# Neighbour sums from PSUM on VectorE, and copies that GpSimd may take

## The chip, the cores and the metric

The kernel runs on one core of a Trainium2 chip. A core has five engines that run side by side and meet at semaphores: TensorE (PE in the profile; PEld is its weight load), VectorE (DVE), ScalarE (ACT), GpSimd (POOL) and SyncE (SP), which here issues the transfers. TensorE writes its results to PSUM, where this kernel has eight tiles of 128 x 512 float32; VectorE and ScalarE read PSUM and the on-chip memory SBUF. The metric is device time in microseconds of one execution; lower is better.

## What is computed

The input is `x` (128 graphs x 128 nodes x 256 features, float32) and `adj` (128 x 128 x 128 integers). Four layers follow one another, each of the form `x = layernorm(x + layer(x, adj))`.

Layer 0 is a gated graph network with three steps:

```
A = (adj != 0)
h = x
for i in range(3):
    m = einsum('bnd,de->bne', h, weight[i])
    aggr = einsum('bst,bsd->btd', A, m)        # neighbour sum
    h = gru_cell(aggr, h, w_ih, w_hh, b_ih, b_hh)
```

The cell forms `gi = aggr @ w_ih.T + b_ih` and `gh = h @ w_hh.T + b_hh`, each three times 256 wide, then `r = sigmoid(i_r + h_r)`, `z = sigmoid(i_z + h_z)`, `n = tanh(i_n + r * h_n)` and `h = (1 - z) * n + z * h`.

Layers 1 to 3 are attention layers: `Wh = x @ W.T`, a score for each pair of nodes from two vectors, leaky ReLU, a mask by `adj`, softmax over the neighbours, and the weighted sum of `Wh`.

## The kernel before

**Tiling.** Four graphs make a group (`G = 4`), so there are 32 groups. Nodes, or features in two halves of 128 (`KC = 2`), lie on the 128 partitions, and a tile's row is usually `GN = 512` float32: four graphs x 128. For each group `gru` does layer 0 and `gat` layers 1 to 3. The product of the adjacency with `h` is formed first (the neighbour sum, L702 in bfloat16 parts or L705 in float32), and the two weight matrices `weight[i]` and `w_ih` are multiplied with each other once near the start (L459), so that a step has two products: hidden state with `whs`, neighbour sum with `wcs[i]`.

**The gates.** These products (`strassen`, matmuls on L639) use Strassen's scheme on 2 x 2 blocks: seven block products instead of eight, whose operands are the blocks themselves or sums of blocks. On the weights' side the sums are made once. On the data's side `sums` makes four tiles of 128 x 256 for the hidden state and four for the neighbour sum, in every step of every group (L608): `second - first`, then `fourth - part(0)`, `fourth - second`, and `part(1) - third`. The second block product of a set waits for all four. The accumulators (`gate`, five PSUM banks) are emptied on the way by `whole` (L716) and `halves` (L720, L723) on ScalarE and by `add` (L644) on VectorE. Then come the nonlinear functions on ScalarE (L734, L747, L763) and the elementwise chain on VectorE and partly GpSimd (L750 to L773).

**The neighbour sum.** Each half is multiplied into one of the three PSUM banks for everything else (`bank`) and copied to SBUF by ScalarE or VectorE (`EVICT`; these instructions carry the lines L404 and L406 of the helper `copy`). `sums` reads these copies.

**Transposes.** Where a tile is turned through the transfer engines' crossbar (`turned`, a DMA transpose of 16-bit elements), float32 words have to be split into 16-bit halves before (`APART`, L404 and L406) and put together after (`TOGETHER`, L503 on ScalarE, L406 on VectorE): 396 such copies of 128 x 1024 in a run. `thirds` splits the hidden state into three bfloat16 parts for the next neighbour sum: roundings (`ROUND`, `copy`) and rests (L528), then crossbar transposes. The last four groups (`LAST = 4`) do without the crossbar and use TensorE's transposes (L803, L860, L907); their stages run side by side at the end of the program.

**Attention.** Scores come from L831 on VectorE, a transpose (L843), a broadcast on GpSimd (L850), a sum with the mask and a maximum (L866), ScalarE's L870 and L887, a transpose of the weights and their scaling (L897, L899), then two products (L937, L948), whose result L954 adds to the layer's input. L555 is a power on GpSimd for the norms, and L582 sums squares.

**Order.** `Plan` is a list scheduler that runs while the program is built. Every operation has the engines that may do it, with a price in ns for each, a priority from its group and stage (`stage`, `LATER`) and buffers from pools with a fixed number of slots. `Plan.order` simulates the engines several times, the later times with due times from the time before, and keeps the shortest plan; the engines' instructions are then issued in that order. Constants in it are `RUSH` (priority of operations that read PSUM), `RATHER` (when GpSimd leaves work to VectorE), `MARGIN` (how long TensorE's operations are kept back after their operands are due from another engine) and `own` (slots that a group's half keeps for itself). Operations with `port=BOTH` are kept apart from each other on VectorE and GpSimd.

Of the kernel before, what the change touches and what calls it, by code (L numbers as in the profile page):

```python
# [20 lines left out]
GN = G * P  # L21
H = GN // 2
# [28 lines left out]
class Plan:  # L51
# [8 lines left out]
             ("ACT", "POOL"): 190, ("ACT", "ACT"): 145, ("DVE", "PE"): 140, ("DVE", "ACT"): 120, ("DVE", "POOL"): 165,  # L60
             ("DVE", "DVE"): 120, ("POOL", "POOL"): 115, ("POOL", "ACT"): 95, ("POOL", "DVE"): 95}

    RUSH = 0.25
    RATHER = 600
    MARGIN = 300

    def __init__(self, slots, own):
        self.free = {t: list(range(n)) for t, n in slots.items()}
# [240 lines left out]
def adj_resnorm_kernel(  # L309
# [14 lines left out]
    nc = tc.nc  # L324
# [9 lines left out]

    pools = {"gru": 4, "xs": 2, "am": 5, "k2": 27, "k4": 18, "f": 3, "mv": 4, "st": 6, "v": 36,
             "mb": 4, "gate": 5, "bank": 3}
    own = ({"k2": 7, "k4": 10, "gate": 0, "bank": 0, "v": 5, "st": 0}, {"k2": 3, "k4": 2, "bank": 0, "v": 4, "st": 0})
    floats = {"gru": 0, "k4": 1024, "xs": 1024, "f": 128, "mv": 8, "st": 6, "v": 4, "mb": GN // 2}
    tags = {t: (n, floats.get(t, 512)) for t, n in pools.items()}
    U16, BF16 = mybir.dt.uint16, mybir.dt.bfloat16  # L340
    BOTH = ("DVE", "POOL")
    LATER = (0.25, 1.75, -1.0, 0.25, 0, -0.5)
    plan = Plan({t: n for t, (n, _) in tags.items()}, own)
    slots = {t: [(psum if t in ("gate", "bank") else work).tile([P, w], F32, name=f"{t}{i}")
                 for i in range(n)] for t, (n, w) in tags.items() if w}
# [1 line left out]
    def T(b):  # L347
        if b.at is None:
            width = 1
            for s in b.shape:  # L350
                width *= s
            at = slots[b.tag][b.slot][:, 0:width]
            if len(b.shape) == 2:
                at = at.rearrange("p (a b) -> p a b", b=b.shape[-1])
            elif len(b.shape) == 3:
                at = at.rearrange("p (a b c) -> p a b c", b=b.shape[-2], c=b.shape[-1])
            b.at = at
        return b.at

    def bank():  # L360
        return Buf("bank", GN)
# [17 lines left out]
    whs = here(consts.tile([P, 7, 3, P], F32, name="whs"))  # L379

    wcs = [here(consts.tile([P, 7, 3, P], F32, name=f"wcs{i}")) for i in range(STEPS)]
# [20 lines left out]
    def copy(e, dst, src):  # L402
        if e == "ACT":
            nc.scalar.copy(dst, src)  # L404
        else:
            nc.vector.tensor_copy(dst, src)  # L406

    LAND = 1500
    EVICT = {"ACT": 475, "DVE": 602}
    APART = {"ACT": 938, "DVE": 602}  # L410
    TOGETHER = {"ACT": 1058, "DVE": 602}
    TURN = -1800
    EVICT2 = {"ACT": 370, "DVE": 350}
    ROUND = {"ACT": 475, "DVE": 335}

    def load(dst, src, prio, start=0):

# [177 lines left out]
                reads=[(ss, b) for b in range(G)] + [eps], writes=[ve], prio=prio, port=BOTH)  # L595
        return ve

    def sums(ms, prio):

        t = Buf("k4", 4, H)  # L600
        first, second = (lambda: T(ms[0])[:, 0:H]), (lambda: T(ms[0])[:, H:GN])
        third, fourth = (lambda: T(ms[1])[:, 0:H]), (lambda: T(ms[1])[:, H:GN])
        part = lambda j: lambda: T(t)[:, j, :]
        for j, (a, b, reads) in enumerate((
                (second, first, [ms[0]]), (fourth, part(0), [ms[1], (t, 0)]), (fourth, second, ms),
                (part(1), third, [ms[1], (t, 1)]))):
            plan.op({"POOL": 690, "DVE": 335}, lambda e, j=j, a=a, b=b: (
                nc.vector if e == "DVE" else nc.gpsimd).tensor_tensor(T(t)[:, j, :], a(), b(), ALU.subtract),  # L608
                reads=reads, writes=[(t, j)], prio=prio, port=BOTH)
        return t  # L610

    def moving(m, ms):
# [52 lines left out]
    def gru(g, stage):  # L665

        xs, am = Buf("xs", G, D), Buf("am", G, P)
        prio = stage(g, 0)
# [4 lines left out]
                writes=[am], prio=prio)  # L673
        if g == 0:
# [3 lines left out]
                reads=[am], writes=[am, turn], prio=prio, port=BOTH)  # L678
        by_thirds = g < NG - LAST
        if by_thirds:  # L680
            low = Buf("mb", GN // 2)
            narrow = lambda b: T(low).bitcast(BF16)[:, b * P:(b + 1) * P]
        if g < 2:
            hT = transposed(xs, lambda b, c: T(xs)[:, b, c * P:(c + 1) * P], prio)
        else:
            hT = [Buf("k2", GN) for c in range(KC)]
            for c in range(KC):
                turned(lambda c=c: T(xs)[:, :, c * P:(c + 1) * P], [xs], hT[c], prio)
        h = None
        for i in range(STEPS):  # L690
            prio = stage(g, i)
            if g == 0 and i > 0:
                input_weights(i, (prio[0], -2))
            agg = []
            for c in range(KC):
                b_, a_ = bank(), Buf("k2", GN)

                def fn(e, b_=b_, c=c, h=h):
                    for b in range(G):
                        if by_thirds and h is not None:  # L700
                            for j in (2, 1, 0):
                                nc.tensor.matmul(T(b_)[:, b * P:(b + 1) * P], h[1](c, b, j), narrow(b), start=j == 2, stop=j == 0)  # L702
                            continue
                        src = T(xs)[:, b, c * P:(c + 1) * P] if h is None else T(h[c])[:, b, :]
                        nc.tensor.matmul(T(b_)[:, b * P:(b + 1) * P], src, T(am)[:, b, :], start=True, stop=True)  # L705
                if by_thirds and h is not None:
                    plan.op({"PE": 12 * 55.6}, fn, reads=[low, h[0][c], h[0][2]], writes=[b_], prio=prio, room=[a_])
                else:
                    plan.op({"PE": 4 * 222.7}, fn, reads=[am, xs if h is None else h[c]], writes=[b_], prio=prio, room=[a_])
                plan.op(EVICT, lambda e, b_=b_, a_=a_: copy(e, T(a_), T(b_)), reads=[b_], writes=[a_], prio=prio)  # L710
                agg.append(a_)
            last = i == STEPS - 1
            h_in, a_in = (whs, (hT, sums(hT, prio))), (wcs[i], (agg, sums(agg, prio)))

            def whole(dst, src, c):
                plan.op({"ACT": 475}, lambda e: nc.scalar.copy(T(dst), T(src)),  # L716
# [12 lines left out]
            for c in range(KC):  # L729

                o, v, d = rz[c], nn[c], Buf("k2", GN)
# [57 lines left out]
            for c in range(KC):  # L789
# [9 lines left out]
                b_ = bank()  # L799
# [223 lines left out]
```

## Time and profile before

| what | before |
|---|---|
| time, median of 3 runs | 2498.13 us (2497.54 to 2498.33) |
| the profiled execution's own time | 2499.11 us |
| its span, first to last instruction | 2497.3 us |
| TensorE busy | 2466.9 us (99%) |
| VectorE busy | 2200.0 us (88%) |
| ScalarE busy | 1896.6 us (76%) |
| GpSimd busy | 1099.4 us (44%) |
| DMA | 161.39 MB, of it 366 crossbar transposes |

The profile shows one execution. A row of its groups has the source line, the engine, the operation, output and inputs by tile name (`k` stands for all work tiles of the pools `k2` and `k4`), shapes and count, then the busy time in us, the mean of one in ns, and the engine's idle time ahead of these instructions with what ended most of it. A line can be that of a helper: all of `copy` is L404 (ScalarE) or L406 (VectorE). A float32 matmul shows as two records.

### The profile page before, as it was taken

The page shows a single profiled execution, that of the slowest core. Times are in us where ns is not written, and L with a number is a line of the kernel's source. Part 1 is how long each engine was busy: PE and PEld are TensorE (multiplying, and loading weights), DVE is VectorE, ACT ScalarE, POOL GpSimd, SP SyncE. Part 2 cuts the span into 40 slices and gives each one's busy share as a digit, 9 for nine tenths or more (in the row PEclk, how much of TensorE's full clock was granted, in tenths as well). Part 3 has the DMA queues.
Part 4 walks back from the last instruction along what each step waited for, and adds up shares of the span by engine and source line. Part 5 has one row for each costly group of instructions (what it writes and reads, how often), then busy time and mean ns, then how long its engine had stood idle before and what let it go on. Part 6 is the DMA issues. An engine that isn't in the chain of part 4 may idle for free. (4 is left out here: it accounts for less than half of the span.)

```text
span 2497.3 us, 42426 instructions
## 1 busy us (share of the span) xinstructions
PE 2466.9 (99%) x13492; PEld 2182.1 (87%) x13492; DVE 2200.0 (88%) x6167; ACT 1896.6 (76%) x4798; POOL 1099.4 (44%) x1312
## 2 busy tenths in 40 slices
PE   9999999999999999999999999999999999999998
PEld 7888888888888888888888888888888888888877
DVE  6888888989989999989988989999999998887887
ACT  5667777878888777777787877777777777776578
POOL 3434445555354543445545445444345543333211
PEclk9999999999999999999999999999999999999999
DMA  5222332333233332433333333232323332210101
GB/s 148 53 54 58 74 75 53 73 72 73 64 85 69 70 74 48 89 76 60 77 68 56 86 66 70 65 84 60 77 60 72 77 72 52 56 26 18 39 1 35
DMA packets 456610, 161.39 MB, mean 65 GB/s; under 512 B 389184, under 2 KB 454720, under 8 KB 456384
## 3 DMA queue, kind: packets, MB, share of 16 engines
q1 hardware_dynamic: 455952, 158.65, 29.6%
q8 instruction: 106, 1.74, 0.3%
q14 instruction: 120, 0.98, 0.1%
q10 hardware_dynamic: 432, 0.01, 0.0%
HBM read 45.89 MB, written 16.78 MB: 25 GB/s over the span
## 5 line engine op out<-in xcount | busy, mean ns | idle before, releaser
L639 PE MATMUL gate<-k,whs 128*128 128x256 f32 x4032 | 1206.5, 381 | 6.0 <-DVE k L644 2.6
L639 PE MATMUL gate<-k,wcs 128*128 128x256 f32 x4032 | 1199.3, 379 | 0.6 <-ACT wcs L404 0.6
L639 PEld LDWEIGHTS gate<-k,wcs 128*128 128x128 f32 x4032 | 766.0, 190 | 105.1 <-ACT wcs L404 1.0
L639 PEld LDWEIGHTS gate<-k,whs 128*128 128x128 f32 x4032 | 740.9, 190 | 111.9 <-DVE k L644 6.9
L644 DVE TENSOR_TENSOR k<-gate,k 128x512 f32<-128x512 f32 x576 | 391.9, 684 | 112.4 <-PE gate L639 85.1
L608 POOL TENSOR_TENSOR k<-k,k 128x256 f32<-128x256 f32 x474 | 399.2, 857 | 174.8 <-ACT k L404 55.9
L555 POOL TENSOR_TENSOR v<-v,neghalf 128x4 f32<-128x4 f32 x128 | 148.8, 1163 | 476.8 <-DVE v L593 232.4
L948 PE MATMUL bank<-gwT,k 128*128 128x256 f32 x1536 | 350.4, 381 | 0.8 <-DVE k L406 0.4
L831 DVE SCALAR_TENSOR_TENSOR nobody<-k,wa 128x256 bf16<-128x256 f32 x768 | 336.9, 471 | 2.7 <-ACT k L574 2.3
L948 PEld LDWEIGHTS bank<-gwT,k 128*128 128x128 f32 x1536 | 289.8, 190 | 41.8 <-DVE k L406 1.7
L608 POOL TENSOR_TENSOR k<-k 128x256 f32<-128x256 f32 x164 | 146.2, 893 | 372.1 <-DVE k L773 107.7
L734 ACT ACTIVATE k<-k,brz 128x512 f32<-128x512 f32 (+1 forms) x384 | 226.3, 623 | 73.9 <-DVE k L644 73.5
L716 ACT COPY k<-gate 128x512 f32<-128x512 f32 x288 | 167.4, 582 | 116.9 <-PE gate L639 113.7
L404 ACT COPY k<-bank 128x512 f32<-128x512 f32 (+1 forms) x283 | 151.0, 536 | 89.6 <-PE bank L843 30.3
L582 ACT ACTIVATE nobody<-k 128x256 bf16<-128x256 f32 x384 | 156.3, 410 | 70.5 <-DVE k L954 69.7
L850 POOL PARTITION_BROADCAST k<-k x336 | 154.1, 558 | 124.4 <-ACT k L404 66.0
L503 ACT COPY k<-k 128x1024 uint16<-128x1024 uint16 x153 | 177.4, 1162 | 33.9 <-DMA k<-k 33.5
L768 POOL TENSOR_TENSOR k<-k,k 128x512 f32<-128x512 f32 x89 | 119.7, 1347 | 188.0 <-ACT k L763 172.7
L954 DVE SCALAR_TENSOR_TENSOR k<-bank,v,k 128x256 f32<-128x256 f32 x384 | 167.4, 476 | 36.1 <-PE bank L948 34.3
L937 PEld LDWEIGHTS bank<-k,k 128*128 128x128 f32 x1536 | 187.8, 193 | 8.6 <-ACT k L503 1.7
L937 PE MATMUL bank<-k,k 128*128 128x128 f32 x1536 | 190.3, 277 | 2.6 <-ACT k L404 1.2
L763 ACT ACTIVATE k<-k,bi 128x512 f32<-128x512 f32 x192 | 137.1, 721 | 39.4 <-DVE k L760 20.2
(109 smaller groups left out, 3472.4 us busy)
## 6 DMA issues: line engine op xcount, KB each, us to landing
xs<-in_x_dram SPq DMA_DIRECT2D x32, 512.0 KB, 4.1
k<-in_x_dram SPq DMA_DIRECT2D x32, 512.0 KB, 4.2
out_dram<-k SPq DMA_DIRECT2D x32, 512.0 KB, 3.0
am<-in_adj_dram SPq DMA_DIRECT2D x32, 256.0 KB, 2.9
k<-k SPq DMA_TRANSPOSE x366, 3.1
k<-in_gnn_wT_dram SPq DMA_DIRECT2D x3, 256.0 KB, 4.9
k<-in_w_ihT_dram SPq DMA_DIRECT2D x2, 384.0 KB, 5.6
k<-in_w_hhT_dram SPq DMA_DIRECT2D x2, 384.0 KB, 6.4
```

Of the source, the lines that this page charges most:

```text
L503: nc.scalar.copy(flat().bitcast(U16).rearrange("p (q h) -> p q h", h=2), T(rows).bitcast(U16).rearrange("p (h q) -> p q h", h=2))
L582: plan.op({"ACT": 400}, lambda e, b=b: nc.scalar.activation(next(nobody[0]), T(y)[:, b, :], AF.Square, accum_out=T(ss)[:, b:b + 1]), reads ...
L608: nc.vector if e == "DVE" else nc.gpsimd).tensor_tensor(T(t)[:, j, :], a(), b(), ALU.subtract),
L639: nc.tensor.matmul(T(dst)[:, j * H:(j + 1) * H], T(w)[:, m, gt, :], moving(m, ms)[1](), start=first and n == 0, stop=n == len(todo) - 1, s ...
L644: plan.op({"DVE": 602}, lambda e: nc.vector.tensor_add(T(o)[:, :, j * H:(j + 1) * H], T(b_).rearrange("p (g n) -> p g n", g=2), T(part).re ...
L716: plan.op({"ACT": 475}, lambda e: nc.scalar.copy(T(dst), T(src)), reads=[src], writes=[(dst, 0), (dst, 1)], prio=prio)
L734: nc.scalar.activation(T(o)[:, gt, n0:n1], src(), AF.Tanh, bias=brz[:, gt * KC + c:gt * KC + c + 1], scale=0.5)
L831: plan.op({"DVE": 345}, lambda e, b=b, h=h, l=l, side=side, xc=xc: nc.vector.scalar_tensor_tensor(next(nobody[1]), T(xc)[:, b, :], 1.0, T( ...
L850: plan.op({"POOL": 292}, lambda e, row=row, b=b, e_=e_: nc.gpsimd.partition_broadcast(T(e_)[:, b, :], T(row)[b * P // G:b * P // G + 1, 0: ...
L937: nc.tensor.matmul(T(b_)[:, b * P:(b + 1) * P], T(xc)[:, b, c * P:(c + 1) * P], T(pT)[:, b, :], start=True, stop=True)
L948: nc.tensor.matmul(T(b_)[:, (b - b0) * D:(b - b0 + 1) * D], T(aT[k])[:, b * P:(b + 1) * P], T(gwT)[:, l, k, :], start=(k == 0), stop=(k == ...
L954: nc.vector.scalar_tensor_tensor(T(y)[:, b, :], T(b_)[:, (b - b0) * D:(b - b0 + 1) * D], T(rden)[:, b:b + 1], T(xc)[:, b, :], op0=ALU.mult ...
```

## The change

`sums` for the neighbour sum now takes its operands from the PSUM banks, apart from the two halves of the first bank where they are subtracted from another operand in PSUM: those come from the copy in SBUF. Only VectorE may do it, without `port=BOTH`, and the tile of sums is allocated together with the matmul. The sums of the hidden state are as before. `copy` gets a GpSimd branch, and the planner may give GpSimd the copies around the crossbar (price 1250) and the roundings to bfloat16 (price 700). Four planner constants differ: `RUSH`, `MARGIN`, one entry of `LATER`, and the `k4` slots of the second half in `own`. Since the planner orders the whole program, the order of instructions differs on every engine. Line numbers after the change are higher: by 2 from `copy` to `sums`, by 3 or 4 from there to the neighbour sum's matmuls, by 5 below.

```diff
--- before.py
+++ after.py
@@ -60,9 +60,9 @@
              ("ACT", "POOL"): 190, ("ACT", "ACT"): 145, ("DVE", "PE"): 140, ("DVE", "ACT"): 120, ("DVE", "POOL"): 165,
              ("DVE", "DVE"): 120, ("POOL", "POOL"): 115, ("POOL", "ACT"): 95, ("POOL", "DVE"): 95}
 
-    RUSH = 0.25
+    RUSH = 1.0
     RATHER = 600
-    MARGIN = 300
+    MARGIN = 200
 
     def __init__(self, slots, own):
         self.free = {t: list(range(n)) for t, n in slots.items()}
@@ -334,12 +334,12 @@
 
     pools = {"gru": 4, "xs": 2, "am": 5, "k2": 27, "k4": 18, "f": 3, "mv": 4, "st": 6, "v": 36,
              "mb": 4, "gate": 5, "bank": 3}
-    own = ({"k2": 7, "k4": 10, "gate": 0, "bank": 0, "v": 5, "st": 0}, {"k2": 3, "k4": 2, "bank": 0, "v": 4, "st": 0})
+    own = ({"k2": 7, "k4": 10, "gate": 0, "bank": 0, "v": 5, "st": 0}, {"k2": 3, "k4": 1, "bank": 0, "v": 4, "st": 0})
     floats = {"gru": 0, "k4": 1024, "xs": 1024, "f": 128, "mv": 8, "st": 6, "v": 4, "mb": GN // 2}
     tags = {t: (n, floats.get(t, 512)) for t, n in pools.items()}
     U16, BF16 = mybir.dt.uint16, mybir.dt.bfloat16
     BOTH = ("DVE", "POOL")
-    LATER = (0.25, 1.75, -1.0, 0.25, 0, -0.5)
+    LATER = (0.25, 1.75, -1.0, 0.25, -0.5, -0.5)
     plan = Plan({t: n for t, (n, _) in tags.items()}, own)
     slots = {t: [(psum if t in ("gate", "bank") else work).tile([P, w], F32, name=f"{t}{i}")
                  for i in range(n)] for t, (n, w) in tags.items() if w}
@@ -402,16 +402,18 @@
     def copy(e, dst, src):
         if e == "ACT":
             nc.scalar.copy(dst, src)
+        elif e == "POOL":
+            nc.gpsimd.tensor_copy(dst, src)
         else:
             nc.vector.tensor_copy(dst, src)
 
     LAND = 1500
     EVICT = {"ACT": 475, "DVE": 602}
-    APART = {"ACT": 938, "DVE": 602}
-    TOGETHER = {"ACT": 1058, "DVE": 602}
+    APART = {"ACT": 938, "DVE": 602, "POOL": 1250}
+    TOGETHER = {"ACT": 1058, "DVE": 602, "POOL": 1250}
     TURN = -1800
     EVICT2 = {"ACT": 370, "DVE": 350}
-    ROUND = {"ACT": 475, "DVE": 335}
+    ROUND = {"ACT": 475, "DVE": 335, "POOL": 700}
 
     def load(dst, src, prio, start=0):
 
@@ -595,18 +597,20 @@
                 reads=[(ss, b) for b in range(G)] + [eps], writes=[ve], prio=prio, port=BOTH)
         return ve
 
-    def sums(ms, prio):
-
-        t = Buf("k4", 4, H)
-        first, second = (lambda: T(ms[0])[:, 0:H]), (lambda: T(ms[0])[:, H:GN])
-        third, fourth = (lambda: T(ms[1])[:, 0:H]), (lambda: T(ms[1])[:, H:GN])
+    def sums(ms, prio, banks=None, t=None):
+
+        t = t or Buf("k4", 4, H)
+        at = banks or ms
+        first, second = (lambda: T(ms[0])[:, 0:H]), (lambda: T(at[0])[:, H:GN])
+        third, fourth = (lambda: T(at[1])[:, 0:H]), (lambda: T(at[1])[:, H:GN])
+        kept = lambda: T(ms[0])[:, H:GN]
         part = lambda j: lambda: T(t)[:, j, :]
         for j, (a, b, reads) in enumerate((
-                (second, first, [ms[0]]), (fourth, part(0), [ms[1], (t, 0)]), (fourth, second, ms),
-                (part(1), third, [ms[1], (t, 1)]))):
-            plan.op({"POOL": 690, "DVE": 335}, lambda e, j=j, a=a, b=b: (
+                (second, first, [at[0], ms[0]]), (fourth, part(0), [at[1], (t, 0)]), (fourth, kept, [ms[0], at[1]]),
+                (part(1), third, [at[1], (t, 1)]))):
+            plan.op({"DVE": 335} if banks else {"POOL": 690, "DVE": 335}, lambda e, j=j, a=a, b=b: (
                 nc.vector if e == "DVE" else nc.gpsimd).tensor_tensor(T(t)[:, j, :], a(), b(), ALU.subtract),
-                reads=reads, writes=[(t, j)], prio=prio, port=BOTH)
+                reads=reads, writes=[(t, j)], prio=prio, port=() if banks else BOTH)
         return t
 
     def moving(m, ms):
@@ -691,9 +695,10 @@
             prio = stage(g, i)
             if g == 0 and i > 0:
                 input_weights(i, (prio[0], -2))
-            agg = []
+            agg, banks, t = [], [], Buf("k4", 4, H)
             for c in range(KC):
                 b_, a_ = bank(), Buf("k2", GN)
+                banks.append(b_)
 
                 def fn(e, b_=b_, c=c, h=h):
                     for b in range(G):
@@ -704,13 +709,13 @@
                         src = T(xs)[:, b, c * P:(c + 1) * P] if h is None else T(h[c])[:, b, :]
                         nc.tensor.matmul(T(b_)[:, b * P:(b + 1) * P], src, T(am)[:, b, :], start=True, stop=True)
                 if by_thirds and h is not None:
-                    plan.op({"PE": 12 * 55.6}, fn, reads=[low, h[0][c], h[0][2]], writes=[b_], prio=prio, room=[a_])
+                    plan.op({"PE": 12 * 55.6}, fn, reads=[low, h[0][c], h[0][2]], writes=[b_], prio=prio, room=[a_, t])
                 else:
-                    plan.op({"PE": 4 * 222.7}, fn, reads=[am, xs if h is None else h[c]], writes=[b_], prio=prio, room=[a_])
+                    plan.op({"PE": 4 * 222.7}, fn, reads=[am, xs if h is None else h[c]], writes=[b_], prio=prio, room=[a_, t])
                 plan.op(EVICT, lambda e, b_=b_, a_=a_: copy(e, T(a_), T(b_)), reads=[b_], writes=[a_], prio=prio)
                 agg.append(a_)
             last = i == STEPS - 1
-            h_in, a_in = (whs, (hT, sums(hT, prio))), (wcs[i], (agg, sums(agg, prio)))
+            h_in, a_in = (whs, (hT, sums(hT, prio))), (wcs[i], (agg, sums(agg, prio, banks, t)))
 
             def whole(dst, src, c):
                 plan.op({"ACT": 475}, lambda e: nc.scalar.copy(T(dst), T(src)),
```

## The prediction

> **What bounds the kernel now.** I read the page's busy shares first, then the lengths of pieces in the chain that ended last, then TensorE's waits in the steady middle, then who waits for the instructions that move. The busy shares and two of the groups:
>
> ```profile
> PE 2466.9 (99%) x13492; PEld 2182.1 (87%) x13492; DVE 2200.0 (88%) x6167; ACT 1896.6 (76%) x4798; POOL 1099.4 (44%) x1312
> ...
> L608 POOL TENSOR_TENSOR k<-k,k 128x256 f32<-128x256 f32 x474 | 399.2, 857 | 174.8 <-ACT k L404 55.9 <-DVE k L773 48.3 <-DVE k L406 18.3
> ...
> L608 POOL TENSOR_TENSOR k<-k 128x256 f32<-128x256 f32 x164 | 146.2, 893 | 372.1 <-DVE k L773 107.7 <-ACT k L404 79.7 <-DVE k L406 73.7
> ```
>
> TensorE is the bound, but its 99% is not its floor, because matmul records overlap. The chain shows long unbroken pieces, which give the pace:
>
> ```profile
> 1839.66 15.54 PE gate L639 x72
> 1855.20 1.78 PE bank L937 x16
> 1856.99 1.73 PE gate L639 x8
> 1858.72 3.45 PE bank L948 x16
> ```
>
> 15.54/72 is 0.216 us for a 256-column matmul record, 1.78/16 is 0.111 for 128 columns; a bf16 record of L702 takes 0.056 (1.34 us x24). Multiplied by the counts: L639 8064 x 0.2158 = 1740; L948 1536 x 0.2156 = 331; L937 and L705 2176 x 0.1113 = 242; L702 1344 x 0.0558 = 75; weights and transposes about 54. Sum 2442 us. The span has 2497.3, so **55 us is all that any reordering could win**: 5.1 before the first matmul, 3.8 lost from there to 50 us, 23 between 50 and 2400 us, 15 from 2400 to the last matmul's end at 2488.9, and 8.4 after it. The change adds and removes no matmul. The middle by what held up a weight load (window 50 to 2400; columns: total us, times, longest):
>
> ```profile
> PEld gate L639 <- DVE k L644: 6.5, 14, 1.4
> PEld gate L639 <- ACT k L716: 5.7, 11, 1.5
> PEld gate L639 <- ACT k L723: 4.2, 12, 1.0
> PEld L702 <- DMA k<-k: 2.2, 6, 0.8
> PEld bank L937 <- ACT k L503: 1.7, 2, 1.5
> ```
>
> The waits are for the copies and sums that empty the gate accumulators. The neighbour sum's additions (L608) are not in the list. Their own view says who waits for them:
>
> ```profile
> who waited for it (us, times):
>   POOL k L608: 6.3, 9
>   DVE k L608: 1.4, 2
> ```
>
> So TensorE waits for none of what is moved to VectorE. It does wait for ScalarE, and the timeline shows one reason: an eviction standing behind a copy around the crossbar.
>
> ```profile
> 1054.27 1.17 ACT L503 COPY k<-k 128x1024 uint16<-128x1024 uint16 x1 [1.60 <-DMA k<-k]
> 1055.34 0.58 ACT L716 COPY k<-gate 128x512 f32<-128x512 f32 x1
> ```
>
> The next gate matmul started at 1055.97, 1.2 us late.
>
> **What the Trainium skill says.** "SBUF — State Buffer", SBUF: two separate sides: VectorE operations with two SBUF inputs and GpSimd operations take one shared port pair by an exclusive lock. The trace fits: DVE's L608, both inputs in SBUF, ranges from 0.40 to 1.50 us. "VectorE: DVE Perf Modes", Why PSUM operands drop a tier: a PSUM operand gets one element per cycle in fp32. That costs a two-input sum nothing here: L757, one input in PSUM, takes 0.415 us, L608 undisturbed 0.40. "GPSIMD Engine Reference", Elementwise — side-by-side cycle accounting: short bodies run at 1.03 cycles per element (1.2 GHz), two-input ones at about 2.6. The trace has no one-input GpSimd copy; its two-input rows go from 0.857 us (256 elements) to 1.232 (512), or 0.48 + 1.46 ns per element.
>
> **The change part by part**, with counts from the order in which the two built programs list their instructions.
>
> *Neighbour sums.* There are 384 (32 groups x 3 steps x 4). Before, 283 stand on GpSimd and 101 on VectorE; after, all 384 are on VectorE, from PSUM. Hidden-state sums stay: 355 and 29 become 351 and 33. VectorE: +384 x 0.415 = +159, and SBUF sums 130 to 33, -97 x 0.63 = -61. GpSimd: -287 x 0.866 = -249. On the path: 0, by the view above. Each PSUM bank is now held until its sums are done. In the built order the next matmul into such a bank stands, after the sums' own cost, mostly 7 us of TensorE work or more later, so I charge 0; without that cover it is two sums, 0.83 us, per reuse.
>
> *Crossbar copies and roundings.* Of 396 crossbar copies ACT/DVE/POOL hold 276/120/0 before, 211/74/111 after; of 252 roundings 187/65/0, then 170/21/61. ScalarE: -32 x 1.162 - 33 x 1.044 - 17 x 0.62 = -82, but it takes 31 more neighbour evictions (x0.585 = 18) and 13 more scalings (x1.6 = 21): -43 us, 2.3% of its 1897. VectorE loses 46 crossbar copies (-34), 44 roundings (-22), 31 evictions (-21), and 34 candidate and other operations (-26): with the sums, 159 - 61 - 103 = -5. It stays at 88%. GpSimd copy price, unknown: estimate from the skill's 1.03 cycles and the trace's fixed 0.48: 1024 elements 1.36 us, 512 elements 0.92. Upper end, the two-input slope: 1.98 and 1.23; lower end, no fixed cost: 0.88 and 0.44. I take the middle: 111 x 1.36 + 61 x 0.92 = 207, and with 21 other tensor operations (+28) GpSimd comes to -14 (-94 to +74), at most 47% busy. The crossbar's DMA count (366) stays; a copy that is 0.3 us longer is hidden, as the matmul behind the score transposes is over 8 us of TensorE work away. Below nothing for the lock: the time that GpSimd holds it hardly changes, so no gain there.
>
> *Planner constants* (RUSH, MARGIN, LATER, the k4 reserve) reorder every engine. This costs no instruction and cannot be priced by row, only by where things now stand.
>
> *Middle, sum.* ScalarE-held waits are 5.7 + 4.2 + 1.7 = 11.6; a quarter of its long crossbar copies go, and with them I take half: -5.8. L644's 6.5 comes from VectorE being late, some of it behind lock-stretched L608; a third: -2.2. Together **-8**. Bounds: nothing gained, or all 18 of these.
>
> *End.* Before, the two last transposes of the hidden state (L803) have 5.7 us of attention matmuls between them and the last gate matmul, and still cost this:
>
> ```profile
> 2407.70 0.66 PE L803 MATMUL bank<-ident,k 128*128 128x128 f32 x4 [0.18 <-DVE k L954]
> 2411.06 0.66 PE L803 MATMUL bank<-ident,k 128*128 128x128 f32 x4 [2.70 <-DVE k L773]
> 2411.55 0.60 PE L907 MATMUL bank<-ident,k 128*128 128x128 f32 x4
> 2413.35 3.78 PE L937 MATMUL bank<-k,k 128*128 128x128 f32 x16 [1.19 <-ACT k L404]
> ```
>
> After, the first stands right behind the last gate matmul and 1.7 us of work separates it from the second. The elementwise chain took 9.6 us (2401.4 to 2411.06), so about 8 us are waited there against 4.1. The deferred matmuls then fill waits that follow, where VectorE is the limit (81 of 97 us): I keep **+2** (0 to +5). Start: same work, other order, 0 (-1 to +1).
>
> Sum: -8 + 2 = -6. The profiled execution took 2499.1 (span and 1.8 around it), 1.0 over the median 2498.1, so 2493.1 in that execution and 2492.0 as a median. A measurement of this kernel tells about 0.2%, 5 us, from no change.
>
> **Rivals.**
>
> *Nothing that TensorE waits for is touched.* For: nobody but L608 waits for L608, DVE stays at 88%, only a few ScalarE waits sit behind crossbar copies. Against: ScalarE's relief is real. Middle -2, end +2: 2498 (2493 to 2503).
>
> *The first product that reads the sums comes to wait on VectorE: slower.* Before, evicting and two GpSimd sums are 0.6 + 2 x 0.86 = 2.3 us; now two VectorE sums are 0.83, with hops about 1.3, and the built order uses that up: of the 96 steps, 28 have less than 3 us of TensorE work between the second bank's matmuls and the first product that reads the last sum (before: 1), five less than 2 us. VectorE issues in order. If three 0.68 us operations stand ahead, the chain is 3.3 us and these 28 wait about 0.7 us, +20; with -2 to -8 elsewhere and +2 at the end, +14 to +20: 2515. It decides once VectorE is over 1.3 us behind in such steps. For: 88% busy. Against: VectorE idles 85 us in 129 waits for gate matmuls before L644, so it is often level with TensorE.
>
> *The change doesn't do what it says* is excluded: the built order has the 384 PSUM sums and 172 GpSimd copies.
>
> **How the numbers follow.** The likeliest case, fewer eviction waits, gives 2492 (2480 to 2493 for this side) and 0.46; no difference, 0.32; the slower side, by late sums or by the end's bare transposes without a gain in the middle, 0.22. The floor on the fast side is -18 with nothing lost, 2480; I go to 2478. On the slow side I go to 2512, most of the late sums.
>
> **What would show it.** Right: L716, L723 and L503 fall by half in the middle's list, POOL copies near 1.36 and 0.92 us, L608's successors from PSUM at 0.415, a wait near 8 us at the last hidden-state transposes. Wrong: TensorE waiting for the new DVE sums, PSUM sums far over 0.415 us, or a middle that still loses 23 us.

## The result and the profile after

| | before | after |
|---|---|---|
| time, median of 5 runs each | 2498.13 us (2497.38 to 2498.53) | 2508.45 us (2507.41 to 2510.63) |
| ratio | 1 | 1.0042, interval 1.003 to 1.0053 |
| span of the profiled execution | 2497.3 us | 2506.7 us |
| lost before the first matmul | 5.1 | 5.1 |
| lost at the start, to the first product of an attention layer | 4.6 | 5.7 |
| lost in the middle, to the last gate matmul | 22.9 | 28.7 |
| lost at the end, to the last matmul's end | 14.6 | 17.0 |
| after the last matmul | 8.5 | 8.5 |

The kernel became slower by 10 us where 6 us less were forecast. "Lost" is worked out from the trace: the distance between the starts of neighbouring matmul records less the pace of the record's kind. The borders are events of the program, so they move with it (the last gate matmul starts at 2401.2 us before and at 2408.1 after). The losses grow by 1.1 + 5.8 + 2.4 = 9.3 us, which is the growth of the span within 0.1. TensorE's work is unchanged. The busy shares on the page of after, and a long late piece of gate matmuls in the chain that ended last:

```profile
PE 2471.2 (99%) x13492; PEld 2182.1 (87%) x13492; DVE 2165.1 (86%) x6298; ACT 1863.7 (74%) x4800; POOL 1064.5 (42%) x1218
```

```profile
1888.72 15.54 PE gate L643 x72
```

The same number of matmuls runs at the same pace (15.54 us for 72 records, as before). VectorE, ScalarE and GpSimd are each busy some 35 us less than before (VectorE 35, ScalarE 33, GpSimd 35), and yet the end comes later: busy time on these three was not what was short.

The groups of after for what was moved, by form (busy us, mean ns, then the idle time ahead), first VectorE, then GpSimd:

```profile
L612 DVE TENSOR_TENSOR k<-bank,k 128x256 f32<-128x256 f32 x288 | 114.6, 416 | 25.5 <-ACT k L404 24.4
L612 DVE TENSOR_TENSOR k<-k,bank 128x256 f32<-128x256 f32 x96 | 39.3, 410 | 0.2
```

```profile
L406 POOL COPY k<-k 128x1024 uint16<-128x1024 uint16 x80 | 102.1, 1280 | 192.5 <-DMA k<-k 63.7 <-ACT k L892 43.8 <-issue 34.4
...
L406 POOL COPY k<-xs 128x1024 uint16<-128x1024 uint16 x31 | 39.1, 1268 | 76.8 <-DMA xs<-in_x_dram 48.1 <-DVE k L773 16.2 <-DVE k L759 5.8
```

All 384 neighbour sums read PSUM, at the price forecast. 111 crossbar copies stand on GpSimd, at 1.27 to 1.28 us. What held up TensorE's weight loads in the middle (window 50 to 2400; total us, times, longest):

```profile
PEld gate L643 <- ACT k L721: 11.2, 17, 2.3
PEld gate L643 <- DVE k L648: 5.1, 10, 1.0
PEld gate L643 <- ACT k L728: 3.1, 7, 1.5
PEld bank L848 <- DVE nobody L836: 1.8, 3, 1.1
PEld bank L942 <- ACT k L505: 1.5, 3, 0.9
PEld bank L942 <- POOL k L406: 0.9, 1, 0.9
PEld gate L643 <- DVE k L612: 0.9, 2, 0.7
```

The waits for ScalarE's whole evictions (L721, L716 before) doubled, from 5.7 to 11.2, on a ScalarE with less to do. For the new sums (L612) TensorE's weight loads wait 0.9 us here. The view of who waits for L612 has the matmuls' own idle time at these events too, and one event at the start:

```profile
who waited for it (us, times):
...
  PEld gate L643: 0.9, 2
  PEld bank L461: 0.7, 1
  PE bank L461: 0.3, 1
  PE gate L643: 0.2, 1
```

The wait of L461, the product of the two weight matrices near the start, is not for a result: at 14.14 us it writes a PSUM bank that the last of a step's four neighbour sums, which ran at 13.67 us, had held until then. It is the one place in this trace where the longer hold of a bank kept TensorE waiting.

The end of after, on TensorE's timeline (start, length, instruction, and in brackets the idle time before it with its releaser):

```profile
2407.86 0.59 PE L643 MATMUL gate<-k,wcs 128*128 128x256 f32 x2
2412.05 1.12 PE L808 MATMUL bank<-ident,k 128*128 128x128 f32 x4 [3.60 <-DVE k L778]
2413.86 1.63 PE L912 MATMUL bank<-ident,k 128*128 128x128 f32 x4 [0.69 <-ACT k L892]
2416.16 2.08 PE L942 MATMUL bank<-k,k 128*128 128x128 f32 x8 [0.68 <-ACT k L404]
2418.03 1.06 PE L808 MATMUL bank<-ident,k 128*128 128x128 f32 x4
```

The first transpose of the last hidden state (L808) stands right behind the last gate matmul, as the built order said, and waits 3.60 us for the elementwise chain.

### The profile page after: what moved, and what is told of

It reads as the page before. It is cut to its first block, busy times and chain, and to the rows that moved or that the text cites. A ratio compares the mean times of both kernels' runs of the same rounds, so it can differ in the third digit from the quotient of the medians.

```text
span 2506.7 us, 42589 instructions
## 1 busy us (share of the span) xinstructions
PE 2471.2 (99%) x13492; PEld 2182.1 (87%) x13492; DVE 2165.1 (86%) x6298; ACT 1863.7 (74%) x4800; POOL 1064.5 (42%) x1218
## 4 chain that ended last, share of the span: by engine, by line
PE 80%; DVE 12%; ACT 4%; DMA 2%; issue 2%; POOL 0%; POOLq 0%; ACTq 0%; SPq 0%; DVEq 0%
PE gate L643 57%; PE bank L953 11%; PE bank L942 6%; DVE nobody L836 3%; PE bank L707 2%; PE bank L710 2%; DMA k<-k 1%; DVE k L648 1%; DVE k L959 1%; ACT k L892 1%; DVE k L871 1%; DVE k L612 1%; DVE k L755 1%; DVE k L408 1%; ACT k L404 1%
## 5 line engine op out<-in xcount | busy, mean ns | idle before, releaser
L953 PE MATMUL bank<-gwT,k 128*128 128x256 f32 x1536 | 350.3, 380 | 2.2 <-DVE k L408 1.1
L953 PEld LDWEIGHTS bank<-gwT,k 128*128 128x128 f32 x1536 | 289.3, 190 | 44.7 <-ACT k L404 3.0
L612 POOL TENSOR_TENSOR k<-k,k 128x256 f32<-128x256 f32 x260 | 222.3, 868 | 112.3 <-DVE k L778 44.7
L739 ACT ACTIVATE k<-k,brz 128x256 f32<-128x256 f32 (+1 forms) x384 | 225.5, 624 | 59.2 <-DVE k L648 58.9
L404 ACT COPY k<-bank 128x512 f32<-128x512 f32 (+2 forms) x315 | 168.1, 539 | 102.4 <-PE bank L942 24.5
L773 POOL TENSOR_TENSOR k<-k,k 128x512 f32<-128x512 f32 x105 | 141.0, 1344 | 241.1 <-ACT k L768 219.1
L721 ACT COPY k<-gate 128x512 f32<-128x512 f32 x288 | 166.5, 579 | 96.6 <-PE gate L643 94.0
L406 POOL COPY k<-k 128x1024 uint16<-128x1024 uint16 x80 | 102.1, 1280 | 192.5 <-DMA k<-k 63.7
L768 ACT ACTIVATE k<-k,bi 128x512 f32<-128x512 f32 x192 | 137.3, 722 | 44.6 <-DVE k L765 25.0
L505 ACT COPY k<-k 128x1024 uint16<-128x1024 uint16 x121 | 140.0, 1162 | 34.9 <-DMA k<-k 31.4
```

What stands on the lines that cost most here:

```text
L739: nc.scalar.activation(T(o)[:, gt, n0:n1], src(), AF.Tanh, bias=brz[:, gt * KC + c:gt * KC + c + 1], scale=0.5)
L953: nc.tensor.matmul(T(b_)[:, (b - b0) * D:(b - b0 + 1) * D], T(aT[k])[:, b * P:(b + 1) * P], T(gwT)[:, l, k, :], start=(k == 0), stop=(k == ...
```

## The experiments

Four things were to be told apart: the sums from PSUM on VectorE, the copies on GpSimd, the planner's constants, and the mere fact that any change gives another order. The last group asks what it is about the sums. All times are medians, and each ratio is against runs of the kernel before taken beside it, whose medians were 2498.1 to 2498.6 us. The losses in the start, the middle and the end are worked out as above.

| kernel | time us | ratio, interval | lost at the start, us | in the middle | at the end |
|---|---|---|---|---|---|
| **neighbour sums as before** | | | | | |
| before | 2498.13 | 1 | 4.6 | 22.9 | 14.6 |
| n_before | 2494.65 | 0.9984, 0.9977 to 0.9991 | 4.8 | 21.6 | 11.2 |
| before_draw3 | 2501.54 | 1.0011, 1.0003 to 1.002 | 5.0 | 21.8 | 17.7 |
| consts_only | 2500.62 | 1.0006, 0.9998 to 1.0015 | 5.0 | 24.0 | 14.7 |
| margin_100 | 2494.74 | 0.9985, 0.9978 to 0.9992 | 4.8 | 18.8 | 12.7 |
| copies_only | 2494.87 | 0.9985, 0.9978 to 0.9992 | 5.1 | 17.9 | 13.7 |
| copies_draw2 | 2499.13 | 1.0003, 0.9994 to 1.0012 | 5.0 | 20.6 | 16.4 |
| copies_margin | 2506.34 | 1.0032, 1.0021 to 1.0044 | 4.9 | 26.5 | 16.9 |
| **all neighbour sums from PSUM on VectorE** | | | | | |
| after | 2508.45 | 1.0042, 1.003 to 1.0053 | 5.7 | 28.7 | 17.0 |
| n_after | 2513.73 | 1.0058, 1.0042 to 1.0075 | 7.0 | 31.6 | 18.5 |
| consts_back | 2505.63 | 1.0026, 1.0015 to 1.0036 | 4.3 | 25.6 | 18.6 |
| no_copies | 2505.17 | 1.0026, 1.0016 to 1.0036 | 5.0 | 25.2 | 17.0 |
| sums_only | 2506.35 | 1.0031, 1.0019 to 1.0043 | 6.2 | 21.4 | 20.7 |
| sums_draw2 | 2508.84 | 1.0044, 1.0029 to 1.0059 | 6.4 | 28.4 | 19.8 |
| **in between** | | | | | |
| tail_as_before | 2503.95 | 1.0023, 1.0014 to 1.0031 | 5.9 | 25.0 | 14.3 |
| all_but_end | 2504.96 | 1.0027, 1.0016 to 1.0038 | 4.6 | 22.5 | 18.0 |
| sums_but_end | 2495.92 | 0.999, 0.9984 to 0.9997 | 6.2 | 18.4 | 12.7 |
| tail_only | 2502.46 | 1.0017, 1.001 to 1.0024 | 4.8 | 25.1 | 16.9 |
| dve_from_sbuf | 2532.29 | 1.0136, 1.0121 to 1.0151 | 5.1 | 52.3 | 18.6 |
| sums_either | 2495.02 | 0.9988, 0.9981 to 0.9995 | 4.6 | 20.6 | 13.4 |

### How much another order alone moves

**n_before**, the kernel before with one price off by 1 ns; **n_after**, the same edit in after; **before_draw3**, another price off by 1 ns in before:

```diff
-    EVICT = {"ACT": 475, "DVE": 602}
+    EVICT = {"ACT": 475, "DVE": 603}   # n_before, n_after, sums_draw2, copies_draw2
+    EVICT = {"ACT": 476, "DVE": 602}   # before_draw3
```

> The kernel before with one planner price raised by 1 ns (VectorE's eviction, 602 to 603), so that nothing but the planner's choices changes. The re-draw theory (the planner turns any small change into another order of the whole program, and orders differ in time by as much as the change did) expects a difference of 3 to 10 us from before, in either direction. The theories that the cause is a part of the change itself (constants, PSUM sums, GpSimd copies) expect within 2 us of 2498.

> The kernel after with the same price raised by 1 ns. Re-draw theory: anywhere between 2497 and 2515, more than 3 us from 2508.4. Theories of a part of the change: the part is still in, so 2508 within 3 us.

> The kernel before with ScalarE's eviction price at 476: a third draw of it. Scatter of the kernels without the sums: 2492 to 2503, with 11 to 15 us lost after the last gate matmul; 2505 or more would take the sums' theory away.

Measured: 2494.65, 2513.73 and 2501.54 us. A nanosecond of price in a planner's table says nothing about the chip, but it changes the order of the whole program, and the time with it: -3.5 us, +5.3 (against after) and +3.4. That is nearly as much as the whole forecast of -6 us. Single kernels of this planner therefore can't carry a claim of a few microseconds; means over several kernels can. The next experiments are read that way.

### The parts alone

**sums_only** is before with the change's `sums`, banks and `room` alone; **sums_draw2** is that with the price of 603; **no_copies** and **consts_back** take the copies or the constants out of after (the diffs in this part are shortened):

```diff
-    APART = {"ACT": 938, "DVE": 602, "POOL": 1250}     # no_copies, from after; the same
+    APART = {"ACT": 938, "DVE": 602}                   # in TOGETHER and ROUND
-    RUSH = 1.0     MARGIN = 200    k4: 1   LATER[4] = -0.5     # consts_back, from after
+    RUSH = 0.25    MARGIN = 300    k4: 2   LATER[4] = 0
```

> The kernel before with the neighbour sums from PSUM on VectorE alone (constants and copies of before). Two planner draws of before stand at 2498.5 and 2494.7, four with the PSUM sums at 2505 to 2514. If the sums are what costs: 2503 to 2508, by longer losses at the end (about 18 us) and in the middle (about 25). If the constants and copies cost and the sums don't: 2492 to 2500.

> The kernel with the PSUM sums alone, and VectorE's eviction price at 603: a second draw of it. Theory that the sums cost by themselves: 2503 or more, with 17 us or more lost after the last gate matmul. Theory that the first draw (2506.35) was chance: below 2501.

> The kernel after without the GpSimd copies (PSUM sums and new constants stay). Theory of the copies ([...]ScalarE waits and so do the evictions behind it): 2498 to 2502, and no small VectorE operation of about 1 us ahead of a long wait of ScalarE. Theory of the constants or of the sums: 2506 to 2512. Re-draw: anything from 2495 to 2512.

> The kernel after (PSUM sums on VectorE, GpSimd copies) with the four planner constants of before (RUSH 0.25, MARGIN 300, LATER entry 0, k4 slots 2). Theory of the constants (less margin lets TensorE reach gate products before ScalarE has emptied the accumulators): back to 2498 or below, with the loss in the middle at 17 us or less and the waits for ScalarE's L721 at 6 us. Theory of the sums or of the copies: stays at 2506 to 2510. Re-draw: anything from 2495 to 2512.

Measured: 2506.35, 2508.84, 2505.17 and 2505.63 us. All four kernels with all neighbour sums on VectorE are slower than before, with or without the copies and the constants. One expectation failed: sums_only lost 21.4 us in the middle, not about 25.

**copies_only** is before with the three POOL prices and the POOL branch of `copy`; **copies_draw2** is that with 603; **consts_only** is before with `RUSH`, `MARGIN` and `LATER` of the change (its `k4` reserve stays at 2, since the planner finds no order with 1); **margin_100** is before with `MARGIN = 100`; **copies_margin** is copies_only with `MARGIN = 100`.

```diff
-    MARGIN = 300
+    MARGIN = 100       # margin_100 and copies_margin
```

> The kernel before with the GpSimd copies and roundings alone. If GpSimd's port time is what costs: 2503 or more. If it is the sums or the constants: 2490 to 2500 (the scatter that a price of 1 ns makes), perhaps at the low end for the relief of ScalarE.

> The kernel with the GpSimd copies alone and the price at 603: a second draw of it. Sums' theory: within the scatter of the kernels without them, 2492 to 2503, with 11 to 15 us lost after the last gate matmul. If the copies themselves gain: 2492 to 2497.

> The kernel before with RUSH 1.0, MARGIN 200 and the LATER entry -0.5; the k4 slots stay at 2, since the planner finds no order with 1. Theory that the constants cost in the middle by waits for ScalarE's evictions of the gates: these waits 12 us or more (before 10.3, its other draw 5.5; kernels with the new constants 14.3, 16.7 and 11.7), time 2499 to 2506. Otherwise waits of 5 to 10 and 2492 to 2500.

> The kernel before with MARGIN 100 alone, twice the step of the change (300 to 200). Theory that MARGIN sets the waits for gate evictions: waits for ScalarE's evictions 15 us or more and for VectorE's L644 over 8, loss in the middle 28 or more, time 2503 to 2512. Theory that it doesn't matter: 2492 to 2500.

> The kernel before with the GpSimd copies and MARGIN 100, neighbour sums as before: two edits that alone gave 2494.9 and 2494.7. If they add up: 2491. If each was one draw of an order near 2496: 2492 to 2499.

Measured: 2494.87, 2499.13, 2500.62, 2494.74 and 2506.34 us. Copies and constants go both ways by the size of the scatter. copies_margin is a plain miss: of two edits that each took 3 to 4 us off, both together added 8. So neither of the two gains was a property of its edit.

The two blocks of the table give the reading. The eight kernels without the sums have a mean of 2498.8 us (standard deviation 4.1), the six with all of them 2508.0 (3.2). **The sums cost 9.3 us**, with a standard error of sqrt(4.1²/8 + 3.2²/6) = 1.9. By stretch it is 0.9 at the start, 5.1 in the middle (21.8 to 26.8, standard error 1.7) and 3.9 at the end (14.7 to 18.6, standard error 1.0). The kernels in a block differ by copies and constants as well as by order, so these are means over such kernels and not repeats of one.

### What it is about the sums

**dve_from_sbuf** puts the neighbour sums on VectorE as the change does, but has them read the copies in SBUF; banks, copies and constants are those of before:

```diff
-    def sums(ms, prio):
+    def sums(ms, prio, engines={"POOL": 690, "DVE": 335}):
...
-            h_in, a_in = (whs, (hT, sums(hT, prio))), (wcs[i], (agg, sums(agg, prio)))
+            h_in, a_in = (whs, (hT, sums(hT, prio))), (wcs[i], (agg, sums(agg, prio, {"DVE": 335})))
```

> The kernel before with all neighbour sums on VectorE, but read from the copies in SBUF as before, so that no bank is held longer. Theory that VectorE's load is what costs (GpSimd's help given up): 2504 to 2515, with the end at 17 us or more and the middle at 24 or more; a little more than with PSUM[...]. Theory that the longer hold of the PSUM banks costs: 2494 to 2501.

Measured: 2532.29 us, 34 more than before, of them 29 in the middle, and far over the expected 2504 to 2515. The group of this kernel on VectorE and what held up TensorE's weight loads in the middle:

```profile
L608 DVE TENSOR_TENSOR k<-k,k 128x256 f32<-128x256 f32 x317 | 143.5, 468 | 3.1 <-ACT k L503 1.6 <-ACT k L404 0.6
```

```profile
PEld gate L639 <- DVE k L644: 11.3, 19, 2.7
PEld bank L843 <- DVE f L835: 6.1, 5, 2.8
PEld bank L937 <- ACT k L503: 4.3, 3, 3.0
```

Again TensorE hardly waits for the sums (1.9 us for L608). It waits for VectorE's other work, the eviction L644 and the attention scores' L835, with VectorE busy at 87%. No bank is held longer in this kernel, so leaving GpSimd out, with VectorE's sums kept apart from GpSimd's work, is what costs in it. The sums from PSUM cost about 34 - 9 = 25 us less. Two things differ there, and were not taken apart: the sum takes 0.41 us against 0.47, and the planner does not keep it apart from GpSimd's work (`port`).

**sums_either** keeps the change's banks, held as long as in the change, but gives the planner the choice for each neighbour sum: VectorE from PSUM, or GpSimd from the copy. The copies and constants are those of before. In the diff against after, `a2` and `b2` are the operands in SBUF, and `extra` has GpSimd's operation read the copies as well as the banks:

```diff
...
-            plan.op({"DVE": 335} if banks else {"POOL": 690, "DVE": 335}, lambda e, j=j, a=a, b=b: (
-                nc.vector if e == "DVE" else nc.gpsimd).tensor_tensor(T(t)[:, j, :], a(), b(), ALU.subtract),
-                reads=reads, writes=[(t, j)], prio=prio, port=() if banks else BOTH)
+            plan.op({"POOL": 690, "DVE": 335}, lambda e, j=j, a=a, b=b, a2=a2, b2=b2: (
+                nc.vector.tensor_tensor(T(t)[:, j, :], a(), b(), ALU.subtract) if e == "DVE" else
+                nc.gpsimd.tensor_tensor(T(t)[:, j, :], a2(), b2(), ALU.subtract)),
+                reads=list(dict.fromkeys(reads + (extra[j] if banks else []))), writes=[(t, j)], prio=prio, port=("POOL",) if banks else BOTH)
```

> The kernel before, with the planner free to give each neighbour sum to VectorE from PSUM or to GpSimd from the copy (it gives most to GpSimd again; the banks are held until the sums are done, as in the change). Theory that GpSimd's lost help costs: like the kernels without the change, 2492 to 2501, with 11 to 15.5 us lost after the last gate matmul. Theory that the longer hold of the banks costs: 2503 or more.

Measured: 2495.02 us; middle and end are back at 20.6 and 13.4. VectorE takes 179 of the 384 neighbour sums from PSUM in it, instead of all:

```profile
L616 DVE TENSOR_TENSOR k<-bank,k 128x256 f32<-128x256 f32 x143 | 58.4, 417 | 9.8 <-ACT k L404 9.0
...
L616 DVE TENSOR_TENSOR k<-k,bank 128x256 f32<-128x256 f32 x36 | 14.9, 413 | 0.4
```

This kernel lies 13 us under the mean of the six, four times their standard deviation. Here the sums that VectorE takes read PSUM and the banks are held until the sums are done, and the cost is gone, so neither of the two costs 9 us by itself. That points to the loss of the choice: all sums must be on VectorE. It is one kernel of this planner, though, and the next part has another, sums_but_end, that is as fast with 336 of the 384 sums bound to VectorE.

### The end

In **tail_as_before** (from after), **sums_but_end** (from sums_only) and **all_but_end** (from consts_back) the last four groups make their neighbour sums as before; **tail_only** (from before) has them from PSUM in these groups alone. `by_thirds` is true for the first 28 of the 32 groups; tail_only has its two cases the other way round:

```diff
-... room=[a_, t])
+... room=[a_, t] if by_thirds else [a_])
-... sums(agg, prio, banks, t)
+... sums(agg, prio, banks, t) if by_thirds else sums(agg, prio)
```

> The kernel after, but in the last four groups (48 of the 384 neighbour sums) the sums are planned as before, from the copies in SBUF and for GpSimd too. Theory of the end (without GpSimd's help in the last groups VectorE's attention work comes too late to stand between the last gate products and the last hidden-state transposes): the first transpose no longer stands bare, loss after the last gate matmul 12 to 15.5 us in place of 17.0, time 2502 to 2506. Theory that all of the loss is in the middle: loss at the end stays at 17 or more, 2506 to 2510.

> The kernel before, with PSUM sums on VectorE in the last four groups alone. Theory of the end: loss after the last gate matmul 17 to 21 us (before 14.6), middle unchanged (18 to 24), time 2500 to 2505. Theory that sums cost only in the middle: 2494 to 2500 with an end of 11 to 15.

> The kernel with the PSUM sums alone, except in the last four groups, whose neighbour sums are as before. Theory of the end: the loss after the last gate matmul falls from 20.7 us to 12 to 15.5, time 2498 to 2503. Theory that the sums cost all along: the end as said, but the middle (21.4 in the first draw) at 25 or more and 2502 to 2508.

> The kernel after with the constants of before, and the neighbour sums of the last four groups as before. Its neighbours are consts_back (2505.63, 18.6 us lost after the last gate matmul) and sums_but_end (2495.92, 12.7 us). Theory of the end: the loss there falls to 11 to 15.5 us and the time to 2494 to 2502. Theory that sums and copies together cost in the middle: middle at 26 us or more and 2502 to 2506.

Measured, end stretch: tail_as_before 14.3 (after 17.0), sums_but_end 12.7 (sums_only 20.7), tail_only 16.9 (before 14.6), all_but_end 18.0 (consts_back 18.6). All four go the way that puts the end's loss down to the last four groups' sums, three of them clearly. The times go the same way: each kernel with the last groups on VectorE is slower than its neighbour without, by 4.5, 10.4, 4.3 and 0.7 us, 5.0 on average. By this mean the last four groups, with 48 of the 384 sums, carry about half of the 9.3 us. For the other 336 sums alone the record is weaker: tail_as_before, sums_but_end and all_but_end have a mean of 2501.6 us, about 3 over the eight kernels without the sums, which is within the scatter of 4.1.

The timelines of TensorE of tail_only and of sums_but_end show what happens at the end:

```profile
2403.16 0.59 PE L643 MATMUL gate<-k,wcs 128*128 128x256 f32 x2
2408.02 1.11 PE L808 MATMUL bank<-ident,k 128*128 128x128 f32 x4 [4.27 <-DVE k L778]
```

```profile
2400.75 3.62 PE L953 MATMUL bank<-gwT,k 128*128 128x256 f32 x16
2404.64 0.66 PE L808 MATMUL bank<-ident,k 128*128 128x128 f32 x4 [0.27 <-DVE k L778]
...
2408.70 1.12 PE L808 MATMUL bank<-ident,k 128*128 128x128 f32 x4 [1.10 <-DVE k L778]
```

In tail_only the transposes stand bare and wait 4.27 us, as in after; in sums_but_end an attention product of 3.62 us stands before them. The traces of all twenty kernels divide in the same way. In the eight whose last groups have all their sums on VectorE (the six of the block, tail_only and dve_from_sbuf), no attention product stands between the last gate matmul and the first of these transposes, which waits 2.9 to 4.3 us. In the other twelve at least 16 matmuls of attention products stand there. The mean loss at the end is 18.4 us in the eight and 14.7 in the twelve. But all_but_end missed its expected 11 to 15.5: it has a product (L953) before the transposes too,

```profile
2403.22 4.03 PE L953 MATMUL bank<-gwT,k 128*128 128x256 f32 x16
2409.27 1.72 PE L808 MATMUL bank<-ident,k 128*128 128x128 f32 x8 [2.01 <-DVE k L778]
```

and loses 18.0 nevertheless, as do before_draw3 (17.7) and copies_draw2 (16.4), where the cover is in place and 11 to 15 were expected. The bare transposes are one way to lose 2 to 4 us at the end and not the only one.

## Why the prediction was wrong, step by step

**Prices and counts held.** The sums from PSUM took 0.410 to 0.416 us (0.415 taken), 153.9 us in all (159). The crossbar copies took 1.27 to 1.28 us (1.36), the 61 roundings 0.71 and 0.84 (0.92), both well inside the bounds. ScalarE came to -33 us (-43), GpSimd to -35 (-14) and VectorE to -35 (-5). Of VectorE's other 30, half is one operation that the prediction left as it was: the 336 sums with the mask that read SBUF (L866, L871 after) took 0.34 us each in place of 0.38, 15 us in all. A slip in the working changes nothing: with the lowest copy prices GpSimd's total comes to about -96, not -94.

GpSimd's copy price was too high for a reason that the traces show. The "0.48 + 1.46 ns per element" was fitted to mean times, and the means contain operations that were held up. The shortest two-input operations of before, 0.716 us for 256 elements (L608) and 1.265 us for 512 (L768), give 2.14 ns per element, the 2.6 cycles that the prediction quotes beside its own slope, and a fixed part of 0.17 us. With 0.17 in place of 0.48 the same estimate gives 1.05 and 0.61 us; the shortest copy and rounding of after took 1.04 and 0.60 us. The means lie above them.

**"On the path: 0, by the view above" is the step that failed.** The term was put at 0 and measured 9.3 us, with a standard error of 1.9, over kernels with and without the sums. The view was read rightly: TensorE waited for no neighbour sum, and after the change its gate matmuls' weight loads wait 0.9 us for two. But the question was not only who waits for the sums; it was also what GpSimd's share of them kept free. With 283 of 384 sums on GpSimd, VectorE was free for something else while GpSimd made them; after, four sums per step must go through VectorE, between its evictions and the attention work. At the end this is seen: with the last four groups' sums on VectorE, no attention product stands before the last transposes, in eight kernels of eight, and about half of the cost lies in these groups. For the other groups it is the likeliest reading and not shown: dve_from_sbuf (+34 us) and sums_either (2495) speak for the loss of the choice, each as one kernel, and sums_but_end (2495.92) against a large cost there. A total of busy time could not tell it: VectorE's was lower after than before.

The step's other half, that the longer hold of the banks costs 0, nearly held: one wait at the start, 0.7 us of weight load.

**"Together -8" in the middle measured +5.8.** Of this the term of ScalarE, "with them I take half: -5.8", went the other way: waits on L716 and L723 were 9.9 us and became 14.3, though ScalarE lost 33 of the 43 us forecast. The term of L644, -2.2, came to -1.4 (6.5 to 5.1). The kernels with the copies and without the sums show that this relief gives nothing to rely on: copies_only, copies_draw2 and copies_margin lose 21.7 us in the middle on average, the other five without the sums 21.8. In the two blocks of the table the gate matmuls' weight loads wait for these evictions 7.7 us on average without the sums (4.9 to 11.3) and 11.7 with them (6.1 to 17.5). This points to ScalarE's evictions coming late because of what VectorE does before them, and one event of after shows such a chain. ScalarE's, VectorE's and TensorE's timelines:

```profile
1510.29 0.46 ACT L752 ACTIVATE k<-gate,bhn 128x256 f32<-128x256 f32 x1
1513.74 0.40 ACT L892 ACTIVATE k<-k,v 128x128 f32<-128x128 f32 x1 [3.00 <-DVE v L888]
...
1514.53 0.56 ACT L721 COPY k<-gate 128x512 f32<-128x512 f32 x1
```

```profile
1511.14 0.99 DVE L884 SCALAR_TENSOR_TENSOR v<-v,v 128x4 f32<-128x4 f32 x1
1512.06 0.68 DVE L755 SCALAR_TENSOR_TENSOR k<-k,k 128x512 f32<-128x512 f32 x1
1512.66 0.99 DVE L888 SCALAR_TENSOR_TENSOR v<-v 128x4 f32<-128x4 f32 x1
```

```profile
1515.14 0.70 PE L643 MATMUL gate<-k,whs 128*128 128x256 f32 x2 [1.84 <-ACT k L721]
```

The eviction L721 stands on ScalarE behind the softmax's L892, which waits 3.00 us for VectorE's small L888; the gate matmul starts 1.84 us late. But the ranges overlap, sums_but_end has 11.6 us of these waits and loses only 18.4 in the middle, and no experiment took this wait alone away. In this event the larger part of the delay is two operations that took 0.99 us each beside a GpSimd copy (see the last section); three neighbour sums had gone through VectorE just before, from 1508.65 us on. That the middle's 5 us are these waits is argued and not shown.

**"End +2" came out at +2.4**, and the transposes stand bare as was said. The size is in part luck: the three waits on the timeline of after come to 3.60 + 0.69 + 0.68 = 5.0 us, not to about 8, against 4.1 before. **Start 0** was +1.1, just over the upper bound of +1.

**The rival for the slow side** (TensorE waits for the sums, +20) had the sign and not the mechanism: those waits are 0.9 us of weight loads. "Nothing that TensorE waits for is touched" fell as well, by its own argument that nobody but L608 waits for L608.

**What the forecast left out** was the planner's scatter, about 4 us either way for a nanosecond of price. With the order unknown, the kernel as built could not be told better than within some 4 us. That the measured 2508.45 lies inside the range is luck: its slow side was drawn mostly for late sums, which did not happen.

Still open: which waits carry the middle's 5 us and whether sums outside the last four groups cost anything clear of the scatter, what besides bare transposes costs 2 to 3 us at some ends, and why two edits like those of copies_margin add up to a loss. Five kernels ran at 2494.65 to 2495.92 us, under both kernels of the case by 0.1%: n_before, margin_100, copies_only, sums_either and sums_but_end. Since one of them is before with a nanosecond changed, none of them shows that its edit is better.

## What to carry to other kernels

An operation for which the bound engine never waits can still be worth its place: ask not only who waits for it, but which engine's order it would have to enter, and what stands in that order with little time to spare. Keep a planner's choice of engine where it has one, and add the cheaper way as an option rather than as a must (sums_either against after: 2495 and 2508 us, one kernel each). Look first at the end of the program, where little other work is left to stand in for a wait: an eighth of the sums carried about half of the cost. Where a planner orders the program, run a few orders that differ by a meaningless nanosecond first; an edit that moves less than they do is not measured by one kernel.

## What the runs showed of the hardware

GpSimd's plain copy cost about half of a two-input operation per element: 1.27 to 1.28 us on average for 128x1024 uint16 (1.04 at the shortest), against 1.34 us for a two-input 128x512 float32 (L773; 1.26 at the shortest). VectorE's two-input sum took 0.41 us with an operand in PSUM and 0.47 from SBUF in dve_from_sbuf, so the PSUM operand was the cheaper one beside a busy GpSimd. The sum with the mask (L866, L871 after) shows the same: 0.284 us with an operand in PSUM in both kernels, 0.380 before and 0.339 after with both in SBUF.

Beside GpSimd's work even the smallest VectorE operations could take several times as long. In the event above GpSimd was copying from 1511.01 us on,

```profile
1511.01 2.63 POOL L406 COPY k<-xs 128x1024 uint16<-128x1024 uint16 x2 [2.54 <-DMA xs<-in_x_dram]
```

and the two operations of 128x4 at 1511.14 and 1512.66 (L884, L888) took 0.99 us each. Of the 192 operations of these two lines in after, the 154 with no GpSimd instruction beside them took 0.15 us on average and at most 0.164. This is not new with the change: in before they took up to 1.23 us beside GpSimd's two-input operations, and the averages did not rise (L888 0.211 us against 0.231). As no_copies, without these copies, was not clearly faster either (2505.17 us), this explains an event and not the 9 us.
